# Products with diagonal matrices in the scan's PSUM banks, and their scans first in a step

## The chip, the cores and the metric

The kernel runs on one core of one Trainium2 chip. Its time is the device time of one launch in microseconds (us). PE stands for TensorE's matmuls, DVE for VectorE, ACT for ScalarE, POOL for GpSimd and SP for SyncE, which issues most of the DMAs. Each engine works through its own instructions in order and waits for the others by semaphores.

## The reference

Two layers over an input of 16 sequences (batches) x 512 positions x 256 features, all in float32. The first layer is a selective scan in both directions; the second a mixture of 16 experts with soft routing. Each adds its input and a layer norm follows.

```python
def _selective_scan(u, dt, A, B, C, D, reverse=False):
    dA = jnp.einsum('bld,dn->bldn', dt, A)
    dB_u = jnp.einsum('bld,bld,bln->bldn', dt, u, B)
    ...
    dA_cum = jnp.exp(jnp.flip(jnp.cumsum(jnp.flip(dA_shift, 1), 1), 1))
    xs = jnp.cumsum(dB_u * dA_cum, 1) / (dA_cum + 1e-12)
    y = jnp.einsum('bldn,bln->bld', xs, C)
    ...
    return y + u * D
```

There are 512 channels (`d`) and 16 states (`n`). The second layer, per sequence: logits against 1024 slots, a softmax over the positions (dispatch) and one over the slots (combine), per expert a gated MLP 256 -> 512 -> 256 over its slots, and the sum over the slots.

## The kernel before

**The scan.** A batch is four calls of `scan_part` (lines 1066 to 1075): two halves of the channels (`p`), each forward and backward (`r`). A part runs over eight pairs of states (`n`, `n + 1`) and in each over two chunks of 128 channels, which makes 16 *steps* a part, 64 a batch and 1024 in all. A step works on tiles of 128 channels x 512 positions, `j` = 0 and 1 being the two states:

- POOL multiplies `du` = dt * u by the states' B, spread over the partitions by DMA (`bs`), into `db` (line 442, three buffers);
- ACT makes the decay exp(A dt) into a PSUM bank of the pool `ps_h` (tag `h`, three banks, line 459) and a factor `th` (line 461, three buffers);
- DVE runs the recurrence in place over that bank (`tensor_tensor_scan`, line 465 forward, 467 backward; below: the scan) and then multiplies it by `th` + 1 into `hg` (line 470, four buffers; below: the multiply), which frees the bank;
- POOL multiplies `hg` by the states' C (`cs`, line 471);
- PE transposes `hg` and adds it up in `acc` (line 386 in `add_up`). It does so two steps behind: `add_up(2)` ends each step. That frees the `hg` buffer.

**Products with diagonal matrices.** For some states (`diag_of`: 3, 7, 11, 15 in the first three batches, 5 and 13 in the others) the product of `du` and B is left to PE. A step that holds such a state (`k` = 1, its `j` = 1) needs only half of `db` from POOL, 128x512 in place of 128x1024. `by_diagonal` multiplies the transposed `du` (`duT`, made by `turn_pair`) by a diagonal matrix of B (`dg`, by DMA) in four matmuls into a bank `hd`, one step ahead. In such a step ACT makes the decay of `j` = 1 in SBUF (`dec`, two buffers), and the scan runs in place over `hd`. ACT takes `j` = 1 first in these steps (line 457), the loop over the scans (line 462) takes `j` = 0 first. There are 304 such products.

**Side work.** All else is cut into pieces that generators yield: the preparation of the next part (`prep`), the out-projection, layer norm and dispatch of the batch before (`front`), experts and combine of pairs of batches (`back`). They share three PSUM banks (`ps`, tag `mps`), which `bank()` hands out in turn and counts in `count`. Before the change `hd` is one of these. `HOLD` in a generator means that its bank still waits to be read; `take_up` lets it do so. `piece` starts a new piece only if the banks from the oldest held one on leave room (`BANKS` = 3); `diags` is the list of the places of products that are not yet consumed and count as held. `beside_scan` runs once a step after the product of the next step is put in. In the last batch (`hurry`) pieces marked `GAP` need not wait a step.

The 8 pairs of experts and the combine of two batches go into `back` at every odd batch from batch 3 on, paced over two batches; in batch 15 over that one. What `back` has left after the last step is done in the tail, together with the last batch's out-projection, dispatch, experts and combine.

**Order.** The code is traced in this order, and a scheduler then sets each engine's order by readiness; what `late` marks stays in program order on its engine.

Of the kernel before, what the change touches and what calls it, by code (L numbers as in the profile page):

```python
# [9 lines left out]
F32 = mybir.dt.float32  # L10
# [7 lines left out]
P = 128  # L18
L = 512
# [36 lines left out]
def seq_layers(tc, ident, neghalf, a, out):  # L56
# [22 lines left out]
    with ExitStack() as ctx:  # L79
# [17 lines left out]
        ps_h = scan_psum.enter_context(tc.tile_pool(name="m_h", bufs=3, space=PSUM))  # L97
# [7 lines left out]
        count = [0]  # L105

        def bank(name):
            count[0] += 1
            if tail and count[0] % 8 >= 3:
                return tail[0].tile([P, 512], F32, tag="tps", name=name)  # L110
            return ps.tile([P, 512], F32, tag="mps", name=name)
# [15 lines left out]
        def late(ins):  # L127

            return tc.keep_in_program_order(ins)
# [150 lines left out]
        def diag_of(b):  # L280

            return (3, 7, 11, 15) if b < 3 else (5, 13)
# [68 lines left out]
        def turn_pair(b, r, p, v):  # L351

            yield 2
            pts = []
            for c in (2 * p, 2 * p + 1):
                pt = bank(f"pdu_{b}_{r}_{c}")
                for lc in range(NL):
                    s = slice(lc * P, (lc + 1) * P)
                    nc.tensor.transpose(pt[:, s], v[c][2][:, s], ident)
                pts.append((c, pt))  # L360
            yield HOLD
            for c, pt in pts:
                duT = p4.tile([P, L], F32, tag="duT", name=f"duT_{b}_{r}_{c}", bufs=2)
                late(nc.scalar.copy(duT, pt))  # L364
                v[c].append(duT)
# [37 lines left out]
        def evict():  # L403
            while evictions:
                evictions.pop(0)()

        def scan_part(b, r, p, v, accs, done, then):

            prep.drain()
            prep.gens += [[1, g] for g in [turn_pair(b, r, p, v)] + then]  # L410
            w, ds = side[r], diag_of(b)
            made = {}

            def by_diagonal(n, c):

                diags.append(count[0])
                made[n, c] = h = bank(f"hd_{b}_{r}_{n}_{c}")
                for lc in range(NL):
                    s = slice(lc * P, (lc + 1) * P)
                    ins = nc.tensor.matmul(h[:, s], v[c][3][:, s], dg[:, s], start=True, stop=True)  # L420
                    if lc == 0:
                        late(ins)

            chunks = (2 * p, 2 * p + 1)
            for n in range(0, NS, 2):
                q = f"{b}_{r}_{p}_{n}"
                k = 1 if n + 1 in ds else 2

                bs = p4.tile([P, 2, L], F32, tag="bs", name=f"bs_{q}")
                cs = p4.tile([P, 2, L], F32, tag="cs", name=f"cs_{q}")  # L430
                nc.sync.dma_start(bs[:, :k, :], v["bc"][0, n : n + k, :].unsqueeze(0).to_broadcast([P, k, L]))
                nc.sync.dma_start(cs, v["bc"][1, n : n + 2, :].unsqueeze(0).to_broadcast([P, 2, L]))
                if n + 3 in ds:
                    dg = p4.tile([P, L], F32, tag="dg", name=f"dg_{q}", bufs=1)
                    nc.sync.dma_start(
                        dg.rearrange("p (l s) -> p l s", l=NL),
                        diag_dram[r, ds.index(n + 3), :, : P * P].rearrange("l (p s) -> p l s", p=P),
                    )
                for c in chunks:
                    dt, rr, du = v[c][:3]  # L440
                    db = p4.tile([P, 2, L], F32, tag="db", name=f"db_{q}_{c}")
                    nc.gpsimd.tensor_tensor(  # L442
                        db[:, :k, :], du.unsqueeze(1).to_broadcast([P, k, L]), bs[:, :k, :], ALU.mult
                    )
                    hg = p4.tile([P, 2, L], F32, tag="hg", name=f"hg_{q}_{c}", bufs=4)
                    hs = {}
                    for j in range(2):
                        if j < k:
                            dec = h = ps_h.tile([P, L], F32, tag="h", name=f"h_{q}_{c}_{j}")
                            hs[j] = (h, dec, db[:, j, :])  # L450
                        else:
                            h = made.pop((n + j, c))
                            dec = p4.tile([P, L], F32, tag="dec", name=f"dec_{q}_{c}", bufs=2)
                            hs[j] = (h, dec, h)

                    ths = {}
                    for j in range(2) if k == 2 else (1, 0):
                        s = slice(n + j, n + j + 1)
                        nc.scalar.activation(hs[j][1], dt, AF.Exp, scale=w["A"][:, c, s])  # L459
                        ths[j] = p4.tile([P, L], F32, tag="th", name=f"th_{q}_{c}_{j}")  # L460
                        nc.scalar.activation(ths[j], rr, AF.Tanh, bias=LN_1E12 / 2, scale=w["Ah"][:, c, s])  # L461
                    for j in range(2):
                        (h, dec, add), th = hs[j], ths[j]
                        if r == 0:
                            nc.vector.tensor_tensor_scan(h, dec, add, 0.0, ALU.mult, ALU.add)  # L465
                        else:
                            nc.vector.tensor_tensor_scan(  # L467
                                h[:, ::-1], dec[:, ::-1], add[:, ::-1], 0.0, ALU.mult, ALU.add
                            )
                        nc.vector.scalar_tensor_tensor(hg[:, j, :], th, 1.0, h, ALU.add, ALU.mult)  # L470
                    nc.gpsimd.tensor_tensor(hg, hg, cs, ALU.mult)  # L471
                    pending.append(
                        (r == n == 0, n == 0, r == 1 and n == NS - 2, c, hg, accs, w, v["u"], f"acc_{q}_{c}", done)
                    )
                    evict()

                    nxt_n = n if c == chunks[0] else n + 2
                    if nxt_n + 1 in ds:
                        for x in sides:
                            x.take_up()  # L480
                        by_diagonal(nxt_n + 1, chunks[1] if c == chunks[0] else chunks[0])
                    beside_scan()
                    if k == 1:
                        diags.pop(0)
                    add_up(2)

        class Side:
# [31 lines left out]
            def piece(self, gaps=True):  # L519

                done = False
                while self.gens and self.hold is None and not self.wait:
                    if self.gap and self.took and gaps:
                        break
                    oldest = min([x.hold for x in sides if x.hold is not None] + diags[:1], default=count[0])
                    if count[0] - oldest + self.need > BANKS:
                        break
                    done = True
                    head = self.gens[0]
                    head[0] = max(head[0] - 1, 1)  # L530
                    fresh = len(head) == 2
                    if fresh:
                        head.append(True)
                    self.go()
                    if not fresh and (not self.gens or self.gens[0] is head):
                        break
                return done
# [11 lines left out]
                    self.piece()  # L549

        hurry = False
        diags = []

        prep, front, back = sides = [Side(), Side(), Side()]

        def beside_scan():
            for x in sides:
                x.take_up()
            prep.piece()
            for x in (front, back) if front.credit > back.credit else (back, front):  # L560
                x.paced_piece(gaps=not hurry)
# [541 lines left out]
@with_exitstack  # L1103
def seq_postln_kernel(ctx: ExitStack, tc: tile.TileContext, a, out):
    nc = tc.nc
    const = ctx.enter_context(tc.tile_pool(name="const", bufs=1))
    ident = const.tile([P, P], F32, name="ident")
    make_identity(nc, ident)
    neghalf = const.tile([P, NSC], F32, name="neghalf")
    nc.gpsimd.memset(neghalf, -0.5)  # L1110
    seq_layers(tc, ident, neghalf, a, out)
# [35 lines left out]
```

## Time and profile before

| | |
|---|---|
| median of three runs | 5326.35 us (5323.48 to 5327.91) |
| the profiled execution, its span | 5322.25 us, 5320.5 us |
| busy PE / DVE / ACT / POOL, us | 4310.4 / 4560.6 / 4104.9 / 4681.6 |
| granted clock of PE, mean | 0.897 |
| a scan of 128x512 on DVE, its multiply | 1.22 us, 0.68 us |
| `db` of both states, of one; `hg` on POOL | 2.36 us, 1.28 us; 2.36 us |
| a product on PE (four matmuls, eight instructions) | 375.7 us busy / 304 = 1.24 us; 1.06 us undisturbed |
| eight transposes into `acc` | 1.04 us back to back |

The span can be cut at the end of every 64th multiplication of `hg` on POOL, which ends a batch: batches 1 and 2 take 283.3 and 284.5 us, the even ones from 4 on 308 to 309, the odd ones from 3 to 13 321 to 327, batch 15 372.6, and what follows the last step 240.4.

Busy times are of one execution. A wait is the idle time of an engine before an instruction, put down to what ended it.

### The profile page before, as it was taken

The page shows a single profiled execution, that of the slowest core. Times are in us where ns is not written, and L with a number is a line of the kernel's source. Part 1 is how long each engine was busy: PE and PEld are TensorE (multiplying, and loading weights), DVE is VectorE, ACT ScalarE, POOL GpSimd, SP SyncE. Part 2 cuts the span into 40 slices and gives each one's busy share as a digit, 9 for nine tenths or more (in the row PEclk, how much of TensorE's full clock was granted, in tenths as well). Part 3 has the DMA queues.
Part 4 walks back from the last instruction along what each step waited for, and adds up shares of the span by engine and source line. Part 5 has one row for each costly group of instructions (what it writes and reads, how often), then busy time and mean ns, then how long its engine had stood idle before and what let it go on. Part 6 is the DMA issues. An engine that isn't in the chain of part 4 may idle for free. (4 is left out here: it accounts for less than half of the span.)

```text
span 5320.5 us, 74550 instructions
## 1 busy us (share of the span) xinstructions
PE 4310.4 (81%) x24498; PEld 3411.1 (64%) x24498; DVE 4560.6 (86%) x6284; ACT 4104.9 (77%) x6573; POOL 4681.6 (88%) x2537
## 2 busy tenths in 40 slices
PE   5677776897778978788788878889787897878889
PEld 3556565676567756676666766667666676657667
DVE  7999999889998899888898888988898889987733
ACT  6777878887888877888887887888778887777644
POOL 6999999989999899999999989998999989988710
PEclk7778888998899989999899988899888998889999
DMA  5444444675446644576446754467544664447545
GB/s 141 137 129 152 126 142 131 211 234 152 146 146 224 222 144 143 171 226 206 132 140 198 236 169 151 134 210 230 157 151 144 217 227 149 144 153 230 168 135 168
DMA packets 614820, 907.82 MB, mean 171 GB/s; under 512 B 84606, under 2 KB 404734, under 8 KB 614432
## 3 DMA queue, kind: packets, MB, share of 16 engines
q1 hardware_dynamic: 532740, 859.35, 50.9%
q10 hardware_dynamic: 81692, 43.70, 3.1%
q8 instruction: 195, 3.19, 0.2%
q14 instruction: 193, 1.58, 0.1%
HBM read 840.34 MB, written 62.56 MB: 170 GB/s over the span
## 5 line engine op out<-in xcount | busy, mean ns | idle before, releaser
L471 POOL TENSOR_TENSOR hg<-hg,cs 128x1024 f32<-128x1024 f32 x1024 | 2416.9, 2364 | 125.0 <-DVE hg L470 108.0
L442 POOL TENSOR_TENSOR db<-du,bs 128x1024 f32<-128x1024 f32 (+1 forms) x1024 | 2087.7, 2042 | 227.8 <-DVE h L465 84.1
L470 DVE SCALAR_TENSOR_TENSOR hg<-th,h 128x512 f32<-128x512 f32 x1744 | 1156.8, 679 | 183.4 <-PE acc L386 105.9
L386 PE MATMUL acc<-ident,hg 128*128 128x128 f32 x8192 | 1163.6, 292 | 106.4 <-POOL hg L471 84.6
L386 PEld LDWEIGHTS acc<-ident,hg 128*128 128x128 f32 x8192 | 1034.4, 152 | 284.6 <-POOL hg L471 131.3
L467 DVE TENSOR_TENSOR_SCAN h<-h,db 128x512 f32<-128x512 f32 x872 | 1044.9, 1219 | 104.9 <-ACT h L459 92.6
L465 DVE TENSOR_TENSOR_SCAN h<-h,db 128x512 f32<-128x512 f32 x872 | 1044.1, 1219 | 44.5 <-ACT h L459 43.6
L461 ACT ACTIVATE th<-rr,Ah_f 128x512 f32<-128x512 f32 x1024 | 724.6, 714 | 200.9 <-DVE hg L470 198.1
L461 ACT ACTIVATE th<-rr,Ah_b 128x512 f32<-128x512 f32 x1024 | 721.3, 712 | 153.5 <-DVE hg L470 143.5
L459 ACT ACTIVATE h<-dt,A_f 128x512 f32<-128x512 f32 x872 | 591.4, 680 | 99.5 <-DVE hg L470 96.3
L459 ACT ACTIVATE h<-dt,A_b 128x512 f32<-128x512 f32 x872 | 592.3, 680 | 85.6 <-DVE hg L470 81.7
L420 PE MATMUL hd<-dg,duT 128*128 128x128 f32 x2432 | 375.7, 305 | 73.2 <-ACT duT L364 27.1
L420 PEld LDWEIGHTS hd<-dg,duT 128*128 128x128 f32 x2432 | 347.9, 220 | 84.5 <-ACT duT L364 29.5
L710 PE MATMUL pl<-x2T,seT 128*128 128x512 f32 x512 | 294.1, 704 | 78.4 <-DVE hg L470 37.4
L838 PE MATMUL peo<-Wd,ht 128*128 128x256 f32 x1024 | 258.1, 408 | 63.2 <-DVE rr L346 36.6
L869 PEld LDWEIGHTS pg<-st,Wg 128*128 128x128 f32 x2048 | 243.1, 195 | 94.1 <-issue 82.8
L811 PE MATMUL pu<-st,Wu 128*128 128x128 f32 x2048 | 255.6, 284 | 49.3 <-DMA Wu<-in_Wu_dram 27.0
L1015 PE MATMUL cpo<-ceo,ct 128*128 128x256 f32 x1024 | 256.0, 407 | 43.2 <-DVE rr L346 40.0
L811 PEld LDWEIGHTS pu<-st,Wu 128*128 128x128 f32 x2048 | 245.9, 199 | 60.6 <-DVE h L467 29.5
L838 PEld LDWEIGHTS peo<-Wd,ht 128*128 128x128 f32 x1024 | 205.5, 206 | 106.1 <-DVE rr L346 39.2
L869 PE MATMUL pg<-st,Wg 128*128 128x128 f32 x2048 | 265.0, 284 | 4.5 <-DMA st<-s_dram 3.4
L1015 PEld LDWEIGHTS cpo<-ceo,ct 128*128 128x128 f32 x1024 | 207.2, 207 | 87.2 <-DVE rr L346 42.7
(165 smaller groups left out, 6754.0 us busy)
## 6 DMA issues: line engine op xcount, KB each, us to landing
cs<-bc SPq DMA_DIRECT2D x512, 512.0 KB, 3.9
bs<-bc SPq DMA_DIRECT2D x360, 512.0 KB, 5.2
Wg<-in_Wg_dram SPq DMA_DIRECT2D x128, 512.0 KB, 5.7
Wu<-in_Wu_dram SPq DMA_DIRECT2D x128, 512.0 KB, 5.8
Wd<-in_Wd_dram SPq DMA_DIRECT2D x128, 512.0 KB, 5.5
dg<-diag_dram SPq DMA_DIRECT2D x152, 256.0 KB, 4.3
bs<-bc SPq DMA_DIRECT2D x152, 256.0 KB, 3.5
x<-in_x_dram SPq DMA_DIRECT2D x32, 512.0 KB, 6.5
```

The source lines that it names most:

```text
L386: ins = nc.tensor.matmul(accs[c][:, s], hc[:, j, s], ident, is_transpose=True, start=False, stop=(last and j == 1 and lc == NL - 1),)
L420: ins = nc.tensor.matmul(h[:, s], v[c][3][:, s], dg[:, s], start=True, stop=True)
L442: nc.gpsimd.tensor_tensor(db[:, :k, :], du.unsqueeze(1).to_broadcast([P, k, L]), bs[:, :k, :], ALU.mult)
L459: nc.scalar.activation(hs[j][1], dt, AF.Exp, scale=w["A"][:, c, s])
L461: nc.scalar.activation(ths[j], rr, AF.Tanh, bias=LN_1E12 / 2, scale=w["Ah"][:, c, s])
L465: nc.vector.tensor_tensor_scan(h, dec, add, 0.0, ALU.mult, ALU.add)
L467: nc.vector.tensor_tensor_scan(h[:, ::-1], dec[:, ::-1], add[:, ::-1], 0.0, ALU.mult, ALU.add)
L470: nc.vector.scalar_tensor_tensor(hg[:, j, :], th, 1.0, h, ALU.add, ALU.mult)
L471: nc.gpsimd.tensor_tensor(hg, hg, cs, ALU.mult)
L811: nc.tensor.matmul(pu[:, fc * P : (fc + 1) * P], got["Wu", e][:, k, fc * P : (fc + 1) * P], st[:, k, :, j * SL : (j + 1) * SL], start=(k = ...
L838: nc.tensor.matmul(po[:, j * DM : (j + 1) * DM], ht[:, fc, :], got["Wd", e0 + j][:, fc, :], start=(fc == 0), stop=(fc == NF - 1),)
L869: nc.tensor.matmul(pg[:, fc * P : (fc + 1) * P], got["Wg", e][:, k, fc * P : (fc + 1) * P], st[:, k, :, j * SL : (j + 1) * SL], start=(not ...
```

## The change

`hd` comes from the scan's pool (`ps_h`, three banks) and no longer from the side work's. With that `diags` goes away in `by_diagonal`, in `scan_part` and in `piece`, and ahead of a product only `prep` takes up what it holds, not all three sides. In steps with `k` = 1 the scans and multiplies run `j` = 1 first.

```diff
             def by_diagonal(n, c):
 
-                diags.append(count[0])
-                made[n, c] = h = bank(f"hd_{b}_{r}_{n}_{c}")
+                made[n, c] = h = ps_h.tile([P, L], F32, tag="h", name=f"hd_{b}_{r}_{n}_{c}")
...
-                    for j in range(2):
+                    for j in range(2) if k == 2 else (1, 0):
                         (h, dec, add), th = hs[j], ths[j]
...
                     if nxt_n + 1 in ds:
-                        for x in sides:
-                            x.take_up()
+                        prep.take_up()
                         by_diagonal(nxt_n + 1, chunks[1] if c == chunks[0] else chunks[0])
                     beside_scan()
-                    if k == 1:
-                        diags.pop(0)
                     add_up(2)
...
-                    oldest = min([x.hold for x in sides if x.hold is not None] + diags[:1], default=count[0])
+                    oldest = min([x.hold for x in sides if x.hold is not None], default=count[0])
```

More of the change, by code (lines that the diff above doesn't have):

```diff
@@ L551, in seq_layers @@
         hurry = False
-        diags = []
         prep, front, back = sides = [Side(), Side(), Side()]
```

## The prediction

> **What bounds the kernel now.** First the page: POOL is busy for 88% of the span, DVE 86%, PE 81%, so no engine alone. I therefore cut the span by batches and asked each stretch for its busy times. The rows are an even batch (4), an odd one (5), batch 15 and what follows the last step; columns are length, then busy time and instructions of PE, its weight loads, DVE, ACT and POOL, then PE's granted clock.
>
> ```profile
> 1224.00:1532.50 308.50, 245.81 (x1283) 186.51 (x1282) 282.83 (x385) 247.80 (x415) 295.09 (x158) 0.88 0.46 140
> 1532.50:1859.00 326.50, 283.94 (x1737) 230.60 (x1737) 283.79 (x397) 262.28 (x400) 295.45 (x158) 0.94 0.67 214
> 4707.50:5080.10 372.60, 313.84 (x1842) 251.86 (x1841) 285.07 (x416) 265.38 (x416) 287.92 (x151) 0.93 0.59 187
> 5080.10:5320.50 240.40, 216.77 (x1216) 177.29 (x1214) 71.71 (x199) 97.36 (x210) 14.68 (x44) 0.97 0.52 160
> ```
>
> DVE and POOL do the same work in both kinds of batch (283 and 295 us). The odd one is 18 us longer because both sit idle: DVE 42.7 us there, 25.7 in the even one. Who holds whom up is in DVE's waits, here of batch 5 (engine, line, for whom: total, times, longest).
>
> ```profile
> DVE hg L470 <- PE acc L386: 13.6, 12, 2.4
> DVE h L467 <- ACT h L459: 5.3, 6, 2.4
> ...
> DVE hd L467 <- PE hd L420: 2.8, 2, 1.9
> ```
>
> DVE never waits for POOL in it, while POOL's waits of the same stretch are for DVE (`db` for the scan 9.9 and 5.6 us, `hg` for the multiply 7.8). The distance is short too: from a step's last multiply to POOL's `hg` of that step the median is 1.6 us in odd batches (k = 1) and 2.1 in even ones, from the trace's starts and ends. So from batch 3 on DVE paces and POOL follows closely. In batches 1 and 2 the same distance is 3 to 4 us, DVE does wait for `db` (6.4 us in batch 1), POOL idles 8 us of 283: there POOL paces. The tail is PE's, 216.8 busy of 240.4 us.
>
> The third view is the tile `hd`: who waited for the instructions that write it or read it.
>
> ```profile
>   DVE hd L467: 40.6, 42
>   PE pl L710: 37.4, 12
>   PE px L686: 30.1, 6
>   DVE hd L465: 21.1, 29
> ```
>
> The first and last are scans that wait for the product, 61.7 us in all. The middle ones are PE's own: side work that cannot have its bank until DVE's multiply has read `hd`. All PE waits on that multiply come to 112 us, some 13 in each even batch, 2 in an odd one.
>
> **Part 1, the side work's banks.** The change ends 108.5 of these 112 us (the rest is before `hd` itself). On DVE I find little behind them: in even batches a wait of 1.3 us for a product and some for ACT. Nothing comes if they hide wholly; at most the 13.3 us by which batch 4 exceeds POOL's 295.1 goes, in six even batches 80. It is nearer nothing, since the 5.0 us PE waits stand where DVE has no gap: I take -2 a batch, -12 in all.
>
> The freed count also lets pieces start earlier. The order of the changed program's instructions has the experts' 6 steps earlier on the mean and the combine's 6 to 7; by mean durations of the groups PE's side work of an odd batch's four parts goes from 50, 47, 65, 50 us to 51, 57, 67, 38. Sums per batch hardly change. A light part is not in itself short: with 47 to 50 us of side work a part takes 77 us in an even batch and 82 in an odd one. Only the last quarter gets clearly lighter. If it falls to the even batches' 77 that is -5 in six batches, -30; if the fuller second and third quarters lose as much, 0 or +15. I take -12.
>
> **Part 2, the tail.** In the changed order three of the four combine pieces of batch 13 stand before the last step and not behind it. In the chain of waits they now lie between the last gate and the normalised output's transposes, with the out-projection (`po`) that the end really needs:
>
> ```profile
> 5088.68 3.45 PE cl L933 x8
> ...
> 5098.74 3.45 PE cpo L1015 x16
> ...
> 5110.69 3.72 PE cpo L1015 x16
> 5114.41 3.45 PE cl L933 x8
> ```
>
> PE's part of a piece is 3.45 (`cl`) + 1.32 (`ctp`) + 3.5 (`cpo`) = 8.3 us, 25 for three. Without them the path is transposes 1.3, copy 0.6, `po` 3.5, two more transposes and copy 1.9, `po` 3.5, add and moments 2, POOL's factors 3.7, ACT 1.9, transposes: it reaches `px` some 19 us after 5088, against 5120.8, so -13, and the logits behind, which wait for a last `cpo`, win 3 to 4 more. From 5160 on PE is 98% busy, so this shift arrives at the end. I take -17, bounds -13 and -25.
>
> **Part 3, batch 15** takes that work: 25 us on PE, and on DVE per piece two maxima 0.69, small ones 0.5, the add 0.48, moments 0.6, about 3 us, 9 for three. There is room on PE (59 idle), but its pieces are chained without a pause (`hurry`) and DVE loses 17 us to late `acc` and 11 to late expert outputs. Side work of its first two parts rises from 55 and 60 to 76 and 72 us, of the third falls from 70 to 59. Bounds 0 and +25; DVE's 9 us lie on the pace: +10.
>
> **Part 4, the scans' new order.** The product is issued at the same place of PE's order as before, behind the transposes of four steps back, in 289 of 304 cases (15 are later). Two things follow.
>
> *Its bank.* The slot frees at the last multiply two steps before the step that uses it. That multiply ended before the product's first matmul in 95% of the products from batch 3 on, and in the median 5 to 8 us before; waits summed over all would be 32 us, on a PE that has more idle time than that. Cost 0, bound +32. ACT's decay of `j` = 0 now waits for a later slot, but its scan is second then: 0.
>
> A rule speaks against exactly this. The Trainium skill, Perfetto Trace Analysis, section Matmuls, says that independent matmul groups should rotate through different PSUM banks, so that one's evacuation overlaps the next one's matmuls; here the products leave a fourth bank for the scan's three. Read as a wait of each product for a scan and a multiply (1.22 + 0.68 us), it would make 304 x 1.9 = 578 us of PE waits. The rows of the last paragraph say that the overlap is kept.
>
> *Its scan.* So far the scan and multiply of `j` = 0 run while PE finishes: 1.9 us of cover. The new order has DVE reach the product's scan earlier, by the scans and multiplies between, on the mean by 0.8 us (first batches), 0.25 (even), 1.25 (odd), 1.6 (batch 15). For each product I took the time from its last matmul to its scan now (median 0.9, 1.5, 0.4 us for the first three kinds) and counted what the earlier place exceeds it by: 10 us a batch in the first three, 5 in even, 13.3 in odd, 14.6 in batch 15, in sum 31 + 30 + 80 + 15. A step in which this goes through whole is this one (1795 to 1806, batch 5): product, both scans, POOL's wait for the step.
>
> ```profile
> 1800.11 1.22 DVE L467 TENSOR_TENSOR_SCAN h<-h,db 128x512 f32<-128x512 f32 x1
> 1801.26 1.06 PE L420 MATMUL hd<-dg,duT 128*128 128x128 f32 x8
> 1801.88 0.68 DVE L470 SCALAR_TENSOR_TENSOR hg<-th,h 128x512 f32<-128x512 f32 x1
> ...
> 1803.13 1.22 DVE L467 TENSOR_TENSOR_SCAN hd<-dec,hd 128x512 f32<-128x512 f32 x1
> ...
> 1805.67 2.37 POOL L471 TENSOR_TENSOR hg<-hg,cs 128x1024 f32<-128x1024 f32 x1 [4.30 <-DVE hg L470]
> ```
>
> DVE would stand still from 1800.11 to 1802.3. The first batches' 31 us hide behind POOL. Of the 125 others, waits of the same steps' multiplies for `acc` go (3.7 us an odd batch, 7.4 in batch 15: 29), since a product stands behind those transposes. Products come in pairs, and a delay at the first is cover for the second: half of 96 is +48. Bounds 0 and +125.
>
> *Its `db`.* In these steps only `j` = 0 uses `db`, and POOL takes the `db` of three steps on ahead of this step's `hg`. Freed by the second scan and not the first, it comes up to 1.9 us later; moving POOL's starts by this, step by step, delays `hg` by 8 us in the first batches, 30 in even, 39 in odd, 9 in batch 15. POOL has 13 and 31 us of idle time a batch to take it up, and DVE does not wait for POOL: +3, bound +86. What is queued behind is `hg` on POOL, then `acc` on PE, two steps from DVE's need.
>
> Two more ACT table loads (348 for 346, 1.28 us each) lie in ACT's idle time: 0.
>
> **Sum.** -12 - 12 - 17 + 10 + 0 + 48 + 3 = +20 us on the profiled execution's 5322.25; the median of the runs is 4.1 higher, so 5326.35 + 20 = 5346 us.
>
> **Rivals.**
> 1. *Faster: the freed banks are worth more and the waits for products less.* For it: 112 us of PE waits, 31 us of POOL idle in an odd batch, and a tail gain that hardly depends on the rest. With -4 in each even batch (-24), -5 in each odd one (-30), the tail -17, batch 15 +10 and a fifth of the 96 us (+19): -42, so 5284 us. Against it: odd batches lose their time to ACT and `acc`, not to the bank.
> 2. *No change.* A quarter of the 96 us (24) against -12 - 12 - 17 + 10 + 3 = -28: 5322 us. What a measurement can tell from no change here is 0.2%, 10.7 us.
> 3. *Much slower: a tightly coupled DVE and POOL pass on all of it.* Products' waits +96, half of late `db` +43, batch 15 +25, tail -17: +147, 5473 us. It decides where waits of scans for products pass 150 us in all from today's 62. Against it: a delay gives PE time.
> That the change does not do what it says is excluded by the order: the products' tiles are in the scan's pool.
>
> **How the numbers follow.** The forecast, slower by 0.2 to 1.4%, 0.48; rival 3 0.10; rival 1 0.29; rival 2 0.13. Slower 0.58, same 0.13, faster 0.29. The forecast's own range is 5337 to 5400. Widened to the side of rival 1 its time is inside: 5280 to 5400; some 0.1 is left out at each end.
>
> **What would show it.** DVE's waits for products at 100 to 150 us (62 now); PE's waits on the multiply for side work gone; a tail of 222 to 227 us and a batch 15 of 375 to 395; odd batches at 327 to 335, even ones near 308. Wrong if odd batches fall below 320, or if scans' waits for products stay near 60.

## Result, and the profile after

The changed kernel takes 5518.95 us (median of four runs, 5515.48 to 5520.48) against 5326.94 us before on the same chip: 1.0361 times, 95% interval 1.0343 to 1.0379. It is slower by 192 us. The forecast of 5346 us, with its range of 5280 to 5400 us, had the sign and missed the size.

The page's first part for the changed kernel, busy time and share of the span by engine, shows that DVE and POOL do the work of before, in as many instructions:

```profile
PE 4363.4 (79%) x24498; PEld 3444.0 (62%) x24498; DVE 4556.9 (83%) x6284; ACT 4122.0 (75%) x6575; POOL 4685.2 (85%) x2537
```

DVE and POOL shares fell from 86% and 88%, since the same work lies in a longer span (5515.8 us for 5320.5). On DVE and POOL all of the added time is idle time. PE is busy 53 us longer (4310.4 before) with the same 24498 matmuls, at a granted clock of 0.880 on the mean for 0.897; whether the lower clock adds to the loss or only comes with it, no run says. The cuts that answer to those of before, again batch 4, batch 5, batch 15 and the tail:

```profile
1270.90:1590.30 319.40, 245.06 (x1284) 187.41 (x1284) 279.68 (x381) 247.42 (x407) 295.30 (x157) 0.87 0.41 133
1590.30:1936.70 346.40, 292.27 (x1732) 233.96 (x1732) 286.58 (x401) 265.94 (x409) 295.61 (x157) 0.90 0.65 204
4921.70:5292.90 371.20, 325.77 (x1896) 261.24 (x1897) 292.15 (x435) 270.01 (x432) 288.18 (x151) 0.94 0.57 185
5292.90:5515.80 222.90, 195.02 (x1122) 162.44 (x1120) 63.42 (x177) 90.10 (x192) 14.60 (x44) 0.95 0.54 170
```

An even batch is 11 us longer, an odd one 20, batch 15 about the same, the tail 17.5 shorter. DVE's busy time in batches 4 and 5 is within 3.2 us of before, so the added time is time in which DVE waits. For what, the waits of the whole run say (engine, line, for whom: total, times, longest), first some of before:

```profile
ACT th L461 <- DVE hg L470: 341.6, 310, 3.2
...
ACT h L459 <- DVE hg L470: 178.0, 183, 5.1
...
DVE hg L470 <- PE acc L386: 105.9, 89, 4.8
```

and then those of the changed kernel:

```profile
ACT h L458 <- DVE hg L469: 472.0, 423, 7.1
ACT th L460 <- DVE hg L469: 235.7, 161, 3.8
POOL db L441 <- DVE h L464: 207.1, 103, 7.1
...
DVE h L466 <- ACT h L458: 162.7, 70, 4.3
...
DVE hd L464 <- PE hd L419: 128.0, 41, 7.4
...
DVE h L464 <- ACT h L458: 89.2, 74, 3.6
...
DVE hd L466 <- PE hd L419: 69.4, 46, 6.1
DVE hg L469 <- PE acc L386: 67.5, 37, 3.7
```

Scans wait 197.4 us for products (128.0 + 69.4), 62 before, and 251.9 us for ScalarE's decays, 136 before. ScalarE itself waits 472.0 us for a bank to be free, 178.0 before. Its waits for a free `th` buffer, which the same multiply frees, fell from 341.6 to 235.7, so that both together rose from 520 to 708. DVE's waits for `acc` fell too (105.9 to 67.5). The waits form a circle, though: ScalarE waits for DVE's multiplies, DVE for ScalarE's decays and TensorE's products. So the runs, not the waits, must say which link was the new one.

### The profile page after: what moved, and what is told of

It reads as the page before. It is cut to its first block, busy times and chain, and to the rows that moved or that the text cites. A ratio compares the mean times of both kernels' runs of the same rounds, so it can differ in the third digit from the quotient of the medians.

```text
span 5515.8 us, 74344 instructions
## 1 busy us (share of the span) xinstructions
PE 4363.4 (79%) x24498; PEld 3444.0 (62%) x24498; DVE 4556.9 (83%) x6284; ACT 4122.0 (75%) x6575; POOL 4685.2 (85%) x2537
## 4 chain that ended last, share of the span: by engine, by line
DVE 38%; PE 25%; ACT 17%; issue 13%; POOL 5%; DMA 3%; DVEq 0%; ACTq 0%; SPq 0%; POOLq 0%
DVE h L464 10%; DVE hg L469 8%; DVE h L466 7%; PE acc L386 4%; ACT h L458 4%; ACT th L460 3%; PE pg L864 3%; PE pq L741 2%; PE peo L833 2%; POOL hg L470 2%; DVE hd L464 2%; PE hd L419 2%; POOL db L441 2%; DVE rr L346 2%; DVE xf L204 1%
## 5 line engine op out<-in xcount | busy, mean ns | idle before, releaser
L386 PE MATMUL acc<-ident,hg 128*128 128x128 f32 x8192 | 1182.6, 295 | 197.9 <-POOL hg L470 116.4
L469 DVE SCALAR_TENSOR_TENSOR hg<-th,h 128x512 f32<-128x512 f32 x1744 | 1149.7, 676 | 142.2 <-PE acc L386 67.5
L466 DVE TENSOR_TENSOR_SCAN h<-h,db 128x512 f32<-128x512 f32 x872 | 1041.5, 1217 | 186.2 <-ACT h L458 162.7
L864 PEld LDWEIGHTS pg<-st,Wg 128*128 128x128 f32 x2048 | 257.9, 205 | 104.0 <-issue 79.3
L928 PE MATMUL cl<-seT,cx 128*128 128x512 f32 x480 | 246.4, 659 | 62.9 <-ACT dis L731 53.8
L464 DVE TENSOR_TENSOR_SCAN hd<-dec,hd 128x512 f32<-128x512 f32 x152 | 184.9, 1217 | 128.2 <-PE hd L419 128.0
L864 PE MATMUL pg<-st,Wg 128*128 128x128 f32 x2048 | 280.3, 294 | 11.4 <-DMA Wg<-in_Wg_dram 7.3
L741 PE MATMUL pq<-dis,xn 128*128 128x256 f32 x1024 | 246.0, 396 | 47.0 <-DVE xf L204 26.1
L705 PE MATMUL pl<-x2T,seT 128*128 128x512 f32 x512 | 257.1, 627 | 27.5 <-ACT sl L751 26.1
```

The lines of the kernel that those rows point to most:

```text
L386: ins = nc.tensor.matmul(accs[c][:, s], hc[:, j, s], ident, is_transpose=True, start=False, stop=(last and j == 1 and lc == NL - 1),)
L466: nc.vector.tensor_tensor_scan(h[:, ::-1], dec[:, ::-1], add[:, ::-1], 0.0, ALU.mult, ALU.add)
L741: nc.tensor.matmul(pq[:, k * 256 : (k + 1) * 256], xn[:, lc, k * P : (k + 1) * P], dis[:, lc, :], start=(lc == 0), stop=(lc == NL - 1),)
L864: nc.tensor.matmul(pg[:, fc * P : (fc + 1) * P], got["Wg", e][:, k, fc * P : (fc + 1) * P], st[:, k, :, j * SL : (j + 1) * SL], start=(not ...
```

## Experiments

Each run's time is compared with the kernel before on the same chip in the same series. The differences in us are medians, this run less its own before.

**Part by part.** The change has three parts that can be made alone: the order of the scans (line 462 of before), the product's bank (line 417), and what the side work does (the count `diags`, and who takes up ahead of the product). In `order_only` only this differs from before:

```diff
-                    for j in range(2):
+                    for j in range(2) if k == 2 else (1, 0):
```

> The kernel before with one edit: in steps with a product its scan and multiply run first. Products stay in the side work's banks, the side work keeps its places. Theory 1 (the order: DVE reaches the product too early): +100 to +190 us against before, waits of scans for products 150 us or more. Theory 2 (the bank: with three slots for decays and products ACT and PE wait for a release) and theory 3 (the side work's new places): within 40 us of before.

5324.31 us, 0.9987 [0.9977, 0.9996]: -7 us. DVE's waits for products rise by only 20 us, from 61.7 to 81.2. The order does not cost, so theory 1 falls.

`no_reorder` is the changed kernel with the old order:

> The kernel after with the scans' old order, j = 0 first. Theory 1: within 60 us of before, so at most 5390. Theories 2 and 3: at least +130 us, 5460 or more; theory 2 has ACT's waits for a bank that DVE's multiply frees stay above 400 us.

5513.21 us, 1.0340 [1.0322, 1.0357]: nearly all of the loss stays without the order.

`bank_only` moves the product's tile alone. The count goes on as if the product still took a bank of the side work's, so that all pieces stay at their steps, and all sides still take up:

```diff
-                made[n, c] = h = bank(f"hd_{b}_{r}_{n}_{c}")
+                count[0] += 1
+                made[n, c] = h = ps_h.tile([P, L], F32, tag="h", name=f"hd_{b}_{r}_{n}_{c}")
```

> The kernel before with the product in the scan's pool and nothing else: the side work's places (the count, the list of products, who takes up) and the scans' order as before. Theory 2: +100 us or more, ACT's waits for banks at 350 to 470 us (178 before). Theories 1 and 3: within 30 us of before; somewhat below is possible, since the PE waits of 112 us for banks that a product holds go.

5428.27 us, 1.0185 [1.0170, 1.0200]: +97 us, just under what theory 2 gave. `bank_order` adds the new order to it:

> The kernel after with the side work's old places: product in the scan's pool, its scan first. Theory 1 or 2: +130 to +200 us, near the kernel after (+192). Theory 3: below +60 us. If it lies more than 40 us above or below the kernel after, the side work's places have that sign and size.

5398.18 us, 1.0129 [1.0114, 1.0144]: +67 us, between the ranges of the theories. It lies 125 us below the changed kernel, so the side work's new places cost 125 us. With a shared bank the new order helps by 30 us. The product's bank then comes free at the step's first multiply and not at its second, which would explain it, though no run shows that alone. The profile of `bank_order`, its waits:

```profile
ACT h L460 <- DVE hg L471: 408.8, 476, 6.1
...
ACT th L462 <- DVE hg L471: 131.3, 149, 3.6
...
PE hd L421 <- DVE hg L471: 77.1, 43, 3.5
...
DVE hd L468 <- PE hd L421: 73.1, 42, 10.3
...
DVE hd L466 <- PE hd L421: 40.0, 20, 4.4
```

Two things could carry the cost: ScalarE's 408.8 us of waits for a bank (173.1 in `order_only`), or TensorE's 77.1 us at the product (3.0).

**The side work's two edits.** `no_count` is `bank_order` without the product's place in the count; `prep_first` is `bank_order` with the count but the narrower take-up:

```diff
-                diags.append(count[0])
-                count[0] += 1
...
-                    if k == 1:
-                        diags.pop(0)
...
-                    oldest = min([x.hold for x in sides if x.hold is not None] + diags[:1], default=count[0])
+                    oldest = min([x.hold for x in sides if x.hold is not None], default=count[0])
```

> The kernel bank_order (product in the scan's pool, its scan first, side work's old places: 5398 us) without the list of products and their count, so that the side work may fill its three banks at any step; all three sides still take up ahead of a product. If the freed count is what costs in the kernel after: 5500 to 5530 us, experts' batches at 345 us, tail 223. If it is that only one side takes up: 5380 to 5420.

5469.58 us, 1.0260 [1.0243, 1.0277]: +140, so 73 more than `bank_order`. That is between the two forecasts. The tail is shorter by 16 us, an odd batch longer by 17 on the mean, the even ones a little shorter: the freed count costs in the odd batches.

```diff
-                        for x in sides:
-                            x.take_up()
+                        prep.take_up()
```

> The kernel bank_order with the other half of the side work's change alone: only the preparation takes up ahead of a product, the count stays. The order of its instructions has the experts later than before (by some 11 to 19 steps) and 138 pieces of side work behind the last step instead of 123. If denser side work costs as the count theory says, thinner side work gains in the steps: batches with experts at or below 330 us and the tail longer by 15 us or more, in sum 5370 to 5420. If the take-up is what costs: 5480 or more.

5433.50 us, 1.0193 [1.0178, 1.0208]: +104, so 37 more than `bank_order`, again between the forecasts. Of these, 27 lie in the tail (267.1 us for 239.9); the odd batches stay as they are (331.3 for 331.9). Both together are the changed kernel (+192): the freed count costs 73 or 88 us, the take-up 37 or 52, as one or the other comes first. Beside the freed count the take-up's 52 us lie in the even batches, 319.3 us in the changed kernel for 310.7 in `no_count`; in batch 4 most of it is in the third quarter (79.8 us for 73.0).

**Which wait makes the bank dear.** First try, `sbuf_decay`: `bank_order`, but in the steps with a product ScalarE's decay and its scan use the free half of `db` in SBUF, so that ScalarE needs no bank there.

```diff
-                            dec = h = ps_h.tile([P, L], F32, tag="h", name=f"h_{q}_{c}_{j}")
+                            if k == 2:
+                                dec = h = ps_h.tile([P, L], F32, tag="h", name=f"h_{q}_{c}_{j}")
+                            else:
+                                dec = h = db[:, 1, :]
```

> The kernel bank_order with the decay of j = 0, in steps with a product, in the half of db that these steps leave free, in SBUF; so a step of this kind takes one of the three banks and not two, as before the change. Side work's old places. If the bank's +70 us come from ACT's decays and PE's products waiting for slots that DVE has not freed: 5310 to 5345 us, ACT's waits for banks below 250 us (409 in bank_order). If they come from the product's place in PSUM as such, or from PE's waits alone: 5370 to 5420.

5848.05 us, 1.0971 [1.0954, 1.0987]. It says nothing of the bank, because DVE's own instructions became slower. The groups of `sbuf_decay` (line, engine, operation, tiles, count | busy us, mean ns of one | idle before it):

```profile
L474 DVE SCALAR_TENSOR_TENSOR hg<-th,db 128x512 f32<-128x512 f32 x304 | 455.8, 1499 | 47.9 <-PE acc L386 36.7 <-ACT th L465 7.1 <-issue 0.4
...
L469 DVE TENSOR_TENSOR_SCAN db<-db 128x512 f32<-128x512 f32 x152 | 356.9, 2349 | 1.9 <-POOL db L443 1.9
...
L474 DVE SCALAR_TENSOR_TENSOR hg<-th,hd 128x512 f32<-128x512 f32 x304 | 204.2, 672 | 3.5
```

The same multiply takes 1499 ns with both inputs in SBUF and 672 with one in PSUM; the scan 2349 ns for 1219.

The second try keeps the scan's result in PSUM and moves only the decay, with the product in the side work's bank (`dec_sbuf_own`, from `order_only`) and in the scan's (`dec_sbuf_ring`, from `bank_order`):

```diff
                             dec = h = ps_h.tile([P, L], F32, tag="h", name=f"h_{q}_{c}_{j}")
+                            if k == 1:
+                                dec = db[:, 1, :]
```

> order_only (5324 us), but in the 304 steps with a product ScalarE's decay of j = 0 goes into the free half of db (SBUF), and only the scan's result into a PSUM bank; the product keeps a bank of the side work's. This is the control for dec_sbuf_ring. Its scan of j = 0 then reads two tiles of SBUF. If SBUF inputs on both sides are what slowed sbuf_decay, that scan takes about 2.2 us instead of 1.22 and the multiply stays at 0.68: 5330 to 5620 us, since not all of 304 us reaches the end. If only a result in SBUF slows, both stay as they are: 5320 to 5335 us.

> bank_order (5398 us) with the same edit: the product shares the scan's three banks, but ScalarE's decay in those steps needs none. bank_order minus order_only was 74 us. Theory A, the bank costs because ScalarE cannot run ahead: the difference to dec_sbuf_own shrinks to 25 us or less, and ScalarE's waits for a bank fall below 250 us from 409. Theory B, it costs because TensorE stands at the product: the difference stays at 55 us or more and TensorE's waits at the product stay near 77 us.

5599.23 us, 1.0507 [1.0491, 1.0523], and 5628.45 us, 1.0562 [1.0546, 1.0578]. The price of the bank shrinks from 74 to 29 us, nearer to theory A's 25 than to theory B's 55; but ScalarE's waits for a bank are 475.3 us and not under 250, TensorE's at the product 41.2 and not near 77, and DVE is again slower. The control shows its scans at 2.3 to 2.4 us with two inputs in SBUF, its multiply unchanged. I count the pair as inconclusive.

Third try, `late_product`: `bank_order`, with the product behind the step's side work and transposes on TensorE.

```diff
-                        by_diagonal(nxt_n + 1, chunks[1] if c == chunks[0] else chunks[0])
                     beside_scan()
                     if k == 1:
                         diags.pop(0)
                     add_up(2)
+                    if nxt_n + 1 in ds:
+                        by_diagonal(nxt_n + 1, chunks[1] if c == chunks[0] else chunks[0])
```

> bank_order (5398 us) with the product issued behind the step's side work and transposes and not ahead of them, so that nothing of the same step is queued behind a product that waits for its bank. Theory B (TensorE standing at the product holds up the transposes and the side work): the time falls to 5330 to 5375 us and TensorE's waits at the product go from 77 us to under 30. Theory A (ScalarE's lookahead): ScalarE's waits for a bank stay near 400 us, the scans' waits for products rise, and the time is 5390 to 5450 us.

5922.12 us, 1.1113 [1.1096, 1.1130], more than either theory gave. TensorE's waits at the product on the multiply are gone (2.5 us), but the scans wait 428 us for the products (113 in `bank_order`). The 527 us above `bank_order` can't be put down to the product's place alone. With it, its entry in `diags` and its step of `count` come later too, and side work finds room earlier: by the order of TensorE's instructions in the traces the experts' pieces stand some 4 steps earlier on the mean than in `bank_order` (5 to 6 in `no_count`). The run does not decide between the theories.

Fourth, `ring_shadow` sets the two apart. From `order_only`: the product goes into the side work's bank as before, and a bank of the scan's is set aside at the place where `bank_order` takes it; the product's scan puts its result there. ScalarE's banks come in the same sequence as in `bank_order`; TensorE waits for none of them. Its instructions come in the order of `order_only` (24486 of 24498 have the same place), and a scan that writes to another bank takes 1.22 us as before.

```diff
-                made[n, c] = h = bank(f"hd_{b}_{r}_{n}_{c}")
+                h = bank(f"hd_{b}_{r}_{n}_{c}")
+                made[n, c] = h, ps_h.tile([P, L], F32, tag="h", name=f"hr_{b}_{r}_{n}_{c}")
...
-                            h = made.pop((n + j, c))
+                            hd, h = made.pop((n + j, c))
...
-                            hs[j] = (h, dec, h)
+                            hs[j] = (h, dec, hd)
```

> order_only (5324 us) with one thing more: the product still goes into a bank of the side work's, but a bank of the scan's three is set aside for it at the same moment as in bank_order, and its scan puts its result there. So ScalarE finds the scan's banks exactly as scarce as in bank_order, while TensorE's product waits for none of them. Theory A (the shared bank costs because ScalarE's decays come later): 5380 to 5410 us, as bank_order's 5398, with ScalarE's waits for a bank above 380 us. Theory B (it costs because TensorE stands at the product): 5315 to 5340 us, as order_only.

5336.77 us, 1.0012 [1.0002, 1.0021]: +7 us, where `bank_order` has +67. Theory A falls: ScalarE's scarcer banks cost 13 us, little more than can be told from nothing, and what is left for the product's own wait is 61. (The side work's bank comes free at the scan here and not at the multiply, 0.68 us earlier; that could hide a little of the 13.) Not all of the 61 need be waiting, for the scheduler also placed some products later: in `bank_order` 12 of the 304 stand one step's transposes further back on TensorE than in `order_only` and `ring_shadow`, six in batch 0 and one in each even batch from 4 on. By the lengths of the batches `bank_order` exceeds `ring_shadow` by 16 us in these and by 49 in batches 1, 2 and the odd ones from 3 to 13, where no product has another place; batch 15 and the tail are 6 us shorter. The waits of `ring_shadow`:

```profile
ACT h L460 <- DVE hg L471: 284.9, 329, 5.7
...
DVE hr L468 <- PE hd L421: 28.1, 38, 1.7
```

With the other line (L466, 16.8 us by the groups of instructions) scans wait 45 us for products, against 113 in `bank_order`. ScalarE's waits for banks, although these are handed out in the same sequence, are 124 us lower, so about half of the rise from 173 to 409 came with the late products. And much of the rise is no added waiting: the multiply that frees a bank also frees a `th` buffer, and ScalarE's waits for those fell, from 380.3 us in `order_only` to 252.4 here and 131.3 in `bank_order`. Both together are 553, 537 and 540 us.

**Where the side work's price comes from.** In the changed kernel TensorE is mostly busy while a scan waits for a product. The timeline of batch 5 (start, length, engine, line; the scan's idle time in brackets) shows a product behind the experts' `pg` and a step's transposes, while the scan has stood for 5.18 us:

```profile
1652.52 1.12 PE L859 MATMUL pg<-ident,bg_rows 64*128 64x512 f32 x2
...
1653.57 2.05 PE L864 MATMUL pg<-st,Wg 128*128 128x128 f32 x16
...
1655.46 1.04 PE L386 MATMUL acc<-ident,hg 128*128 128x128 f32 x8
...
1656.33 1.06 PE L419 MATMUL hd<-dg,duT 128*128 128x128 f32 x8
...
1657.43 1.23 DVE L464 TENSOR_TENSOR_SCAN hd<-dec,hd 128x512 f32<-128x512 f32 x1 [5.18 <-PE hd L419]
```

I summed what TensorE did in all waits of over 0.5 us for a product, from the trace's starts and ends with each matmul cut at the next one's start. Before, of 53 us, 40 were the product's own matmuls, 5 transposes and 6 idle. In the changed kernel, of 190 us, 57 were the product, 62 transposes, 32 `pg` and 17 `px`. Counted in the same way, the side work among the two steps' transposes that stand ahead of an odd batch's product is no larger (7.3 us on the mean, before and after), but of another kind: `pg` 72 us in all odd batches before and 200 after (72 in `bank_order`, 170 in `no_count`), `peo` 144 and 41. (The `pg` figures in the expectation below are sums of the matmuls' full durations, which overlap, and so larger.)

Two runs keep side work out of single steps of the changed kernel and make up for it in the others; some of it goes into the tail (235.6 and 231.5 us for 222.9). Batch 15 (`hurry`) is left as it is. `rest_k1` rests in the steps with a product (`beside_scan(k == 1)`), `rest_ahead` in the two steps whose pieces stand ahead of the products:

```diff
-                    beside_scan()
+                    beside_scan(n + 3 in ds)
...
-                if self.credit >= 1.0 and self.piece(gaps):
+                if self.credit >= 1.0 and not rest and self.piece(gaps):
```

> The changed kernel (5519 us) with the side work of experts, combine and gate left out of the steps that have a product and made up for in the steps behind; prep's pieces stay. Theory S1, the 85 to 121 us that the side work's new places cost come from side work that now stands in the steps with a product, between the product before and the next: 5430 to 5480 us, odd batches at 330 to 339 instead of 346.7, waits of scans for products 110 to 150 instead of 197 us. Theory S2, they come from fuller stretches whatever the step: 5500 to 5540 us, odd batches 343 to 352.

> The changed kernel (5519 us) with the experts', the combine's and the gate's pieces left out of the two steps whose side work stands ahead of the next products on TensorE, and made up for in the others. Theory S1, the side work's new places cost because longer pieces (the experts' pg, 461 us of PE time ahead of the odd batches' products against 221 in bank_order) stand ahead of the products: waits of scans for products fall from 197 us to under 120 and odd batches from 346.7 to 330 to 340 us; time 5430 to 5490 us. Theory S2, the density of side work costs wherever it stands: the waits for products fall too, but waits for ScalarE rise by as much, odd batches 344 to 352 us, time 5500 to 5640 us as for rest_k1 (5627).

5626.92 us, 1.0559 [1.0541, 1.0576], and 5612.51 us, 1.0533 [1.0517, 1.0549]. In both the scans' waits for products fell as theory S1 has it (118.6 and 98.3 us from 197.4), and in both the time rose by some 100 us: other waits took their place. In `rest_ahead`, where POOL also waits 171.3 us for the multiply, they are these:

```profile
ACT h L458 <- DVE hg L469: 540.5, 431, 7.1
...
PE hd L419 <- DVE hg L469: 143.6, 84, 5.2
```

TensorE, with less in front of it, reaches the product before its bank is free (31.3 us of such waits in the changed kernel). The odd batches become 355.8 us, more than theory S2 allowed too. In `rest_k1` they are 345.1, hardly less than 346.7 though the waits for products fell by 79 us; its loss lies in the even batches (333.9) and in batches 2 and 15. S1 as a cure is refuted, and S2 has its sign but not its size.

**A mixture.** `last_batch` uses the new order in batches 0 to 14 and the whole change in batch 15 only, to have the shorter tail without the loss:

```diff
-                diags.append(count[0])
-                made[n, c] = h = bank(f"hd_{b}_{r}_{n}_{c}")
+                if hurry:
+                    h = ps_h.tile([P, L], F32, tag="h", name=f"hd_{b}_{r}_{n}_{c}")
+                else:
+                    diags.append(count[0])
+                    h = bank(f"hd_{b}_{r}_{n}_{c}")
+                made[n, c] = h
...
-                        for x in sides:
+                        for x in [prep] if hurry else sides:
...
-                    if k == 1:
+                    if k == 1 and not hurry:
```

> A version that may beat both: the kernel order_only (5324 us) in batches 0 to 14, the kernel after in batch 15, where the freed count lets the combine of batch 13 leave the tail. Expected: batch 15 at 365 to 372 us, tail 222 to 224 for 240, in sum 5300 to 5312 us, 0.3 to 0.5% below before.

5330.47 us, 1.0000 [0.9991, 1.0010]. The tail is 9.6 us shorter and batch 15 is 15 longer than in `order_only`: the work is moved, at most, and nothing is won. None of the runs beats the kernel before by more than `order_only`'s 0.13%.

Lengths from the ends of each batch's last `hg` on POOL, in us (batches 1 and 2; means of even and odd ones from 3 to 14). They are those of the profiled execution, which lies up to 5 us from the median that the second column is made from:

| kernel | time less before | 1, 2 | even | odd | 15 | tail |
|---|---|---|---|---|---|---|
| before | 0 | 283.3, 284.5 | 308.4 | 325.7 | 372.6 | 240.4 |
| order_only | -7 | 285.4, 287.7 | 308.4 | 326.4 | 369.7 | 240.4 |
| ring_shadow | +7 | 282.3, 287.5 | 309.5 | 326.1 | 369.8 | 240.6 |
| bank_order | +67 | 290.8, 293.3 | 311.7 | 331.9 | 364.6 | 239.9 |
| prep_first | +104 | 290.8, 301.5 | 313.8 | 331.3 | 363.1 | 267.1 |
| no_count | +140 | 289.7, 290.8 | 310.7 | 348.7 | 368.8 | 223.5 |
| after | +192 | 291.3, 294.7 | 319.3 | 346.7 | 371.2 | 222.9 |
| rest_ahead | +282 | 288.8, 315.0 | 318.4 | 355.8 | 387.1 | 231.5 |
| rest_k1 | +299 | 283.3, 308.2 | 333.9 | 345.1 | 381.5 | 235.6 |
| last_batch | +1 | 285.8, 287.7 | 308.4 | 326.5 | 385.0 | 230.8 |

Read downwards from before over `order_only`, `ring_shadow`, `bank_order` and `no_count` to after, the steps are -7 (order), +13 (a bank set aside from ScalarE's three), +61 (the product written there, with its wait and the 12 later places), +73 (count), +52 (take-up): 192 us.

## Why the prediction was right or wrong

**What bounds the kernel** held from batch 3 on as far as the waits show: what DVE waits for there is ScalarE and TensorE, and POOL in only some 3 us of an even batch (20.4 us for POOL's `hg` in the whole run). For batches 1 and 2 it was wrong: there POOL was to hide DVE's waits, yet both became 8 to 10 us longer.

**Part 1**, "I take -2 a batch, -12 in all" and again "I take -12" for the earlier places. This is the step that failed most: the earlier places, put at -12 us (with -17 for the tail and +10 for batch 15 it makes -19), cost 125 us, with the tail's gain already in it: the freed count 73, by longer odd batches, and the narrower take-up 52, by longer even ones. TensorE's 108.5 us of waits for side banks did go (none are left in the changed kernel), and nothing came of it: that half of the step was right in saying that DVE has little behind them. The other half judged by how much side work each quarter of a batch holds, and put the loss in the second and third, with a lighter fourth. Measured, the four quarters of an odd batch went from 80.9, 82.1, 80.7, 82.0 us to 88.4, 88.1, 86.0, 84.1. All grew, the first most, though its load was to change by 1 us. What changed is the kind of the pieces near the products: with a bank more in hand a long `pg` goes ahead of a product where the count had kept it back. So the count was perhaps also a brake. How much of the 125 us runs through this, how much through ScalarE and how much through the lower clock stays open: the two runs that moved the pieces away lost more elsewhere. Nor does a run say by what wait the take-up lengthens the even batches.

**Part 2** was right: -17 forecast, -17.5 measured.

**Part 3** took +10 for batch 15; it is 1.4 us shorter. By the table the freed count adds 4 us to it and the take-up 2, within the bounds of 0 and +25, while the order and the shared bank had made it 8 shorter (364.6 us in `bank_order`); why, no run says, nor why all of the change in batch 15 alone makes it 385.0 (`last_batch`).

**Part 4, its bank**: "Cost 0, bound +32". It costs 74 us beside the new order and 97 beside the old. The working took the multiply that frees the bank and the product's first matmul from the trace of before, found the one earlier in 95% of cases, and summed TensorE's waits to 32 us. In `bank_order` TensorE waits at 43 of 304 products, 77 us where the working had summed 32, and what a late product costs comes on top: scans that wait for it, and behind them the multiply that frees the next bank. A margin read where nothing depends on it did not hold once its two ends were tied together. The rule of the Trainium skill (Perfetto Trace Analysis, section Matmuls) that independent matmul groups should rotate through different PSUM banks, weighed and set aside in the prediction, has the direction right: with the product left in its own bank the rest of the sharing costs 13 us, with the product in the shared one 74. The 578 us of TensorE waits that the reading of it gave is far too much: 77 us were measured.

**Part 4, its scan**: "half of 96 is +48". The order alone gives -7 us, and -30 where the bank is shared; with the side work's new places it is +10, which the intervals do not tell from nothing. The halved sum of missing cover was no price: in `order_only` the waits for products rose by 20 us, where it had counted 125 from batch 3 on; those for decays rose by 30, and those for `acc` and `th` fell by 25.

**Its `db`**, +3: POOL's waits for the scan rose from 130 to 314 us in the changed kernel, but in `order_only` only to 156 and with no loss. Nothing shows a price of its own.

**The rivals.** Rival 3, the tightly coupled DVE and POOL at 5473 us with waits for products past 150 us, was the nearest: 197 us, and 5519. But its source was to be the order, and that is not the source. What the prediction set as the mark of error happened in neither form: odd batches did not fall, the waits did not stay near 60; odd batches went past 335 and even ones past 308, beyond what it said would show it right.

## What to carry to other kernels

When a tile moves into a pool that another engine already turns over, do not read the margin of its new wait from the old trace: there the two ends are free, and afterwards a late one can make the next later. A count that limits how far side work runs ahead can be worth more than the bank that it protects; before freeing it, look at what it keeps out of the queue in front of the critical instruction. And separate the parts of an edit by a stand-in, as the bank set aside but not written by TensorE, before believing the largest wait: here 409 us of waits on ScalarE came with a price of 13 us, since some of them were the effect of late products and some had only moved from one buffer to another.

## What the hardware showed

A scan or multiply on DVE takes about twice as long on the mean when both inputs lie in SBUF. In `dec_sbuf_own` only the decay's place differs between these groups; both write to PSUM:

```profile
L469 DVE TENSOR_TENSOR_SCAN h<-h,db 128x512 f32<-128x512 f32 x720 | 861.8, 1217 | 118.2 <-ACT h L461 109.7 <-POOL hg L473 5.6 <-POOL db L442 2.2
...
L469 DVE TENSOR_TENSOR_SCAN h<-db 128x512 f32<-128x512 f32 x152 | 364.6, 2410 | 0.7 <-ACT db L461 0.2
```

The added 1.15 us on 304 scans are some 350 us of DVE, and the kernel is 278 us slower than `order_only`. What makes the difference is whether POOL is at work when the scan starts: by the trace's starts and ends the 261 of these scans that start while POOL runs take 2.56 us on the mean, the 43 others 1.21 us, none over 1.24. The multiply of `sbuf_decay` takes 1.89 us in 206 cases and 0.68 us in 98. Before, with the decay in PSUM, 1581 scans started while POOL ran, and took 1.22 us. A stretch of `sbuf_decay` shows it beside POOL (start, length, engine):

```profile
2007.17 1.20 DVE L469 TENSOR_TENSOR_SCAN db<-db 128x512 f32<-128x512 f32 x1
2007.40 3.13 POOL L443 TENSOR_TENSOR db<-du,bs 128x1024 f32<-128x1024 f32 x1 [2.38 <-issue]
...
2009.46 2.15 DVE L469 TENSOR_TENSOR_SCAN db<-db 128x512 f32<-128x512 f32 x1
...
2010.49 3.26 POOL L475 TENSOR_TENSOR hg<-hg,cs 128x1024 f32<-128x1024 f32 x1
...
2011.54 2.77 DVE L474 SCALAR_TENSOR_TENSOR hg<-th,db 128x512 f32<-128x512 f32 x1
```

Each length fits an instruction that begins its work only when the other engine's is done. POOL's `db` starts 0.97 us before the first scan's end: 0.97 and its mean of before, 2.37, make 3.34, and it takes 3.13. The second scan starts 1.07 us before that `db` ends: 1.07 + 1.22 = 2.29, measured 2.15. POOL's `hg`: 1.12 + 2.36 = 3.48, measured 3.26. The multiply: 2.21 + 0.67 = 2.88, measured 2.77. The sums are 0.1 to 0.2 us too long each time. The Trainium skill (SBUF — State Buffer, section Who interferes with whom) says that a VectorE instruction with two inputs in SBUF contends with a GpSimd instruction that reads SBUF, through a port that one of them holds for its whole length, whereas one with at most one such input does not; the runs agree, at 2.41 against 1.22 us on the mean for the scan and 1.50 against 0.67 us for the multiply. That is what PSUM is worth to this kernel's scans: the decay in a bank keeps DVE and POOL apart.
